# A four-layer graph transformer on one core: row sums taken from two key tiles added by an accumulating DMA, with one mask, one pool of large buffers and a new order table

## The chip, the core and the metric

The kernel runs on one core of one Trainium2 chip. A core has five engines with a queue each: TensorE (matmuls, PE in the profile), VectorE (DVE), ScalarE (ACT), GpSimd (POOL) and SyncE (SP, which here only issues transfers). Sixteen DMA engines move data between HBM and the on-chip memory SBUF, or within SBUF. Each queue runs in its own order; engines wait for one another through semaphores. The metric is the device time of one execution in microseconds (us).

## The reference, cut to what matters

Sixteen graphs of 1024 nodes with 256 features pass four attention layers that share one adjacency matrix. Layers 0, 1 and 3 are graph attention layers, layer 2 is a transformer layer. Only layer 2's attention is touched in its way of computing:

```python
# x: (16, 1024, 256), adj: (1024, 1024) int32, zeros and ones
h = jnp.maximum(_layernorm(x, axis=-1), 0.0)
x = x + _L0_gnn_ref(h, adj, W, a)            # masks with adj == 0
h = jnp.maximum(_layernorm(x, axis=-1), 0.0)
x = x + _L1_gnn_ref(h, adj, W, a)            # masks with adj > 0
h = jnp.maximum(_layernorm(x, axis=-1), 0.0)
x = x + _L2_gnn_ref(h, adj, ...)
...
def _L2_gnn_ref(x, adj, ...):                # 8 heads of 32 features
    scores = jnp.einsum('fnhd,fmhd->fhnm', q, k) / jnp.sqrt(D)
    scores = jnp.where(adj > 0, scores, -1e9)
    attn = jax.nn.softmax(scores, axis=-1)
    t = jnp.einsum('fhnm,fmhd->fnhd', attn, v).reshape(F, N, C)
    x = _layernorm(x + t, ln1_g, ln1_b)
    f_out = relu(x @ w1 + b1) @ w2 + b2
    return _layernorm(x + f_out, ln2_g, ln2_b)
```

The softmax is computed without subtracting a maximum: the exponentials are multiplied by a 0/1 mask, the weighted values and the sums of the weights are accumulated apart, and the values are multiplied by the inverse of the sums at the end.

## The kernel before

The kernel works in 64 stages, one for each layer and graph. `order` interleaves them so that the stages of different graphs fill one another's gaps: (2, b), (1, b+1), (3, b), (0, b+2) in the middle of the run. Everything that an engine does is laid down as an `op` with its engine, an assumed cost, what it comes after, and the buffers (`Hold`) that it takes and ends. `play` then plays all of them against those assumed costs and emits them in that order. Which op is preferred where several could go next comes from `RANKS`, a table of three characters for each op written out in the source. So the order of each queue is fixed when the kernel is built, by the table, the assumed costs and the number of buffers in each `Ring`.

A layer 2 stage has 32 items, one for each half of the queries `n` (512 of them), group of four heads `g` and key tile `j` (128 keys). `dot_item` lays one down:

- `scores` (L1522): four matmuls of 32 x 128 by 32 x 512 into two double banks of PSUM, one for each head (in the profile each f32 matmul appears as two instructions);
- two exponentials on ScalarE (L1536), two heads each, PSUM to the buffer `pe` in SBUF, 128 x 2048 f32, 1 MB;
- two multiplications by the mask on VectorE (L1544), in place;
- `values` (L1556): four matmuls, 32 columns each, that add v-transposed times `pe` into the bank `acc`, over the eight key tiles;
- in the same op the sums (L1561): four matmuls with `pick` as weights, 32 columns, column `g` ones and the others zeros, that add the column sums of `pe` into the bank `sums`, over the eight key tiles and both groups.

After the last key tile of a half, `dot_out` copies `acc` and `sums` to SBUF, transposes them (tps, tpo, L1587), inverts the sums, scales, adds into y (L1621, GpSimd), and `feed_forward` follows. Layer 3 (`pair_item`) has the same two kinds of matmul (L1402 values, L1426 sums), with its weights p2 from VectorE (L1368). Layers 0 and 1 use `gat_item` (av, L1312, weights L1295).

The large buffers of 1 MB lie in three rings: "p" with 4 (the weights), "big" with 4 (qT, kT of layer 2, r2 of layer 3), "y" with 2. Two masks of 128 x 8 x 1024 bytes, 1 MB each, are built at the start by `mask_of`: `mask_nz` (adj not zero, layer 0) and `mask_pos` (adj greater than zero, the others), each from 8 compares on VectorE (L1762, with a count of the neighbours, `degree`), 64 transposes on TensorE (L1768) and 8 copies on ScalarE (L1772). At the end some seen values are checked; if one is out of bounds a general path computes everything again, which these inputs do not need.

GpSimd's queue holds the inverse roots of the layer norms (L1010, L1011), adds into x and y, and before the change no transfer; nearly all transfers are issued on SP: x in (L623), out (L1501), the rows of source terms out to HBM (L1238, L1241) and back, spread over the partitions (L1252, L1257).

Of the kernel before, what the change touches and what calls it, by code (L numbers as in the profile page):

```python
# [28 lines left out]
U8 = mybir.dt.uint8  # L29
# [18 lines left out]
    "#&P#%+#&C#(I####%@#$p##d#$Y#%L#$g#%]#%q#&B#&3#&]#%M#'S#&`#'%#'Z#'q#&]#&T#%0#'[#'T#'>#(&#'j#(>#)W#)?#);#(X#)d#*$"  # L48
    "#(_#(##)6#);#'m#)=#)L#*x#)K#)W#)N#*0#*i#+@#)w#*m#,/#,h#,C#+[#+U#,p#,:#-P#,1#%8#&A#'b#$l#(N#%t#%>#&_#'N#%]#&Y#%Z"
    "#%{#'0#'q#%4#&6#'0#&[#&6#(j#&V#%F#'s#'T#'H#&F#(]#%x#'D#&(#%e#'Z#&{#&F#'i#&m#'9#'x#&W#'^#(6#'`#'>#'E#'g#'3#'@#(+"  # L50
    "#'8#(-#'D#*7#(V#(7#%/#?7#*X#'R#'>#'}#%V#)w#([#)<#+##<9#,@#Dm#B5#Db#EG#EA#,d#0v#)j#+s#&R#&i#(;#'W#(8#)3#(>#(R#'e"
    "#(q#):#(s#)6#+4#+7#+/#%z#)]#)u#).#(+#+'#*Y#*E#)?#+8#)@#(=#*1#,+#*M#+U#*0#+F#*|#+q#,$#+L#*8#+O#,;#+|#+9#-7#.|#,b"
    "#,O#.s#+W#.`#+-#.2#([#(b#(Y#)V#)_#*,#)z#(M#)Y#*A#*G#,-#.Y#,##/(#,f#+/#+r#+7#,f#.5#-)#)G#*A#,1#-:#-4#-?#-{#,[#.A"
    "#,|#+z#,R#-1#+G#-P#-|#.E#-w#05#)w#._#/W#/0#/7#.f#-}#-;#/u#-N#2`#Pu#41#0s#/]#0s#2k#1J#*D#*]#'-#'2##Z#)]#(@#*z#*M"
    "#(3#).#-)#(i#*E#(:#+r#*z#-o#2W#*B#,H#+T#&/#*:#);#+g#*J#,D#(t#)o#$+#){#+-#+1#)&#)U#*E#'w#*Q#)j#(N#'E#+@#,v#,^#*q"
    "#.T#';#)F#*j#+T#)c#-o#+I#,L#+P#GC#.h#).#*1#+t#,7#.8#,t#.M#,z#.e#//#11#/S#/]#-[#+w#+T#0J#/t#,;#.+#/%#-2#,f#,2#+E"
    "#3b#.o#.Q#/>#.)#0;#.`#.W#-d#36#.7#.+#02#0]#0t#0w#2T#1,#.>#1s#1_#4D#,X#04#16#0`#6S#2J#2r#1c#5|#0C#2O#2+#0K#-5#/{"
    "#.H#.w#-s#,Y#1S#3P#1G#1##1y#-O#0##2$#1C#1{#1=#1l#3n#2*#4P#3l#.=#2-#/a#27#2^#5+#25#0L#/c#2p#1r#0V#2d#5@#0T#4,#2N"
    "#42#4p#4p#4:#3_#33#5R#1J#3%#3+#e=#2(#5x#6$#5k#6M#8a#28#.:#0%#/n#-E#5e#4)#5%#/@#21#4l#2D#1<#4$#3d#2=#0r#2O#2*#2V"
    "#2p#/O#6/#-a#,(#3-#3N#4[#3^#49#8y#6%#41#4q#2*#12#0g#7]#18#5v#59#4}#6{#4]#3:#7d#4k#7r#2[#5C#2k#/t#2%#31#2&#3m#7e"  # L60
    "#3*#6Q#0P#3^#6-#4p#7f#27#4g#1,#5x#5*#6_#4N#5U#1k#7*#6z#52#8T#4]#7b#7`#3B#7k#7d#5E#6b#7Y#58#6##:,#5o#:j#:o#7Z#<:"
    "#83#:Q#;v#6|#6]#5{#4o#7##9i#7)#4S#9K#5o#7)#7.#88#=B#9k#1P#7V#4k#54#9e#7*#;W#9^#6Q#5f#7.#7)#:(#6C#6_#9T#6[#8h#9S"
    "#7&#<Q#6P#<F#:4#9b#8U#8i#8h#58#<F#=+#>7#5)#4L#7z#7-#:p#6m#9;#8Z#:u#;c#6W#<##:s#:T#<_#<{#<C#8t#:0#=>#<V#;*#;+#:6"
    "#9l#7M#<V#<k#=Z#:T#<Q#8J#7=#<:#88#Ac#;r#;j#=7#:A#;l#=g#=v#8t#;l#<t#>d#@?#='#:a#>X#<Y#=Q#=;#<e#A8#<&#9p#=R#=}#;Z"
    "#;F#9r#>L#@8#>B#=r#>1#90#=x#=z#?+#<j#?g#AL#@H#=f#?5#=t#<N#=u#;m#@%#@)#?+#?l#As#<p#?z#>V#?e#<_#BS#<W#@##Ar#?e#<]"
    "#;@#B{#?V#Bf#A(#?=#@W#At#?f#B8#B'#AF#EX#C0#A<#@f#Bg#A7#=*#@x#D7#BX#AY#Av#>o#DZ#C<#CI#C'#@V#@1#Ax#B_#AQ#CH#Ad#@i"
    "#BU#B$#DN#Cw#B)#@<#E0#BX#Ca#Eq#Dr#BU#EQ#C?#DO#EB#ED#Eb#F$#E>#F@#EL#Dw#Do#Ei#EF#Dq#Et#Ei#G$#Ei#Ff#FU#GK#I0#Fo#H+"
    "#FR#HB#H[#F0#HS#G^#JX#Ix#G)#Iy#J&#I0#J|#KV#JL#He#I`#Iy#KF#Ij#IY#M6#J0#Fm#G<#G[#KS#L7#O;#JJ#IJ#Mf#Km#MG#M4#LA#J{"
    "#KD#M9#K'#NN#Ln#Lz#M]#O+#OH#BO#BS#DY#AJ#C]#F)#Bq#B.#DY#D6#Dh#E[#B@#Ax#Dm#BX#CZ#EE#DG#E/#CO#CD#E0#BF#Db#G7#FK#C/"
    "#F(#EP#D|#D1#GB#FX#FP#F+#C%#>]#E9#CG#Fa#H2#Gn#GI#GX#FQ#FE#G4#H+#Eu#F/#Fi#EY#Gp#H;#Gk#E>#G&#I9#J+#H_#E:#Jw#Ht#Fy"  # L70
    "#H]#J>#EU#H9#H*#J,#H]#I(#J7#Ir#GQ#JL#I3#K,#G<#GF#J##I?#IR#K+#II#G}#IP#II#J?#IL#Ip#Mp#I9#Ho#E-#K.#JH#IM#KX#IY#K$"
    "#KN#K.#IU#Jf#KT#Lg#J^#KH#Jm#Kn#Jt#Jg#Ln#JN#K,#KM#Jd#I$#Ho#Nf#Mm#K1#N;#Me#LG#Mj#LU#M=#Oo#Pj#Jp#KE#O+#MD#N=#NC#Ld"
    "#LB#LY#NJ#NP#N.#OV#O}#N=#M%#OF#NO#N0#N;#O;#Om#OS#Pw#O_#O3#OR#M@#GZ#Mx#P.#JA#L3#PY#O7#Qf#OZ#NF#qD#Rw#Ot#QT#Yr#SN"
    "#|Q#>A#?E#99#;_#>G#:q#=]#?$#?,#6c#?B#<v#>W#<0#>9#Ax#=M#<z#<{#?f#=y#AF#AL#A/#@'#Cz#@p#@]#?5#@l#<l#AJ#BO#<i#@5#Cs"
    "#;?#?G#CN#=f#>'#=5#@j#A<#B+#@`#<w#E'#B[#Bk#DQ#BF#Af#Cd#D1#B>#lz#Ha#Bz#BA#HQ#JB#Mn#Fe#I]#J8#Ia#JV#IT#KW#Jg#L2#Im"
    "#Kt#M?#M7#Pn#P4#Q6#Ns#Is#N9#Qh#M]#OL#J/#N.#Io#PW#NR#MS#NQ#S=#JD#SW#Nq#Np#LG#Nt#N{#MN#LS#Q<#Qf#S_#Pp#P/#S_#N5#N'"
    "#Qw#TH#Nu#No#R8#MC#LI#MU#Q<#K|#Mb#LR#M9#L:#LK#OJ#O4#Q-#Pt#MM#Py#OW#S6#O%#NW#LM#O)#O(#QB#P_#P$#NY#St#Mr#L`#Or#Pa"
    "#Le#R5#O3#P>#O##R>#Q-#P5#OR#P)#Mr#Vx#Mh#RU#Q:#P|#RP#QN#P+#Sr$&C#_o#MW#Po#d:#_P#cS#P1#Qo#H]#Kc#O}#OP#Rx#NX#Qy#S,"
    "#R?#R,#QA#O&#Nq#Q4#X7#P`#S)#TD#SG#Tv#T[#Wm#T7#OP#Rh#Tq#Xv#UD#Q{#Te#Te#Ut#Ui#Wo#N_#TP#LF#RQ#Uq#RM#RX#Sf#VZ#Pd#Rc"
    "#TK#Q'#T*#R^#T9#U=#W3#R3#W?#U8#RR#UL#SU#]d#U}#VD#VW#VJ#Wb#Xv#eo#eE#p}#Wu#e|#ii#jv#ju#Y%#SG#W5#Ur#VY#T<#UF#W9#Sj"  # L80
    "#Ur#V-#[j#V+#U{#X5#Zq#Wh#Y-#TW#T0#WN#YD#Zi#Z-#WL#WX#X;#YO#Z9#XI#XG#Uo#[n#Y*#WC#ZV#Wc#Wi#_f#Xk#W<#Vp#W-#WY#T<#Yb"
    "#XD#[D#[X#Vc#X+#VR#YH#Qa#W_#Yu#V`#YZ#Vr#U`#[4#YN#Y$#^f#Zs#Y9#X$#Y>#Z8#Zm#W%#[J#Y'#V?#ZR#^X#ZV#Y|#ZJ#Ww#T/#^G#QI"
    "#^1#[;#Z0#[}#ZU#Z}#Z<#_h#WJ#Y$#[?#Z9#[r#^{#]]#Z+#]+#[|#ZD#^*#a5#Z^#Z5#^%#^M#]L#^a#]n#^g#]d#_r#^Y#]x#Yu#^p#]|#[W"
    "#^J#`1#aF#_n#ag#aE#bw#b.#b5#c<#c1#e/#a:#`+#^x#^^#`c#cZ#eB#`@#a^#c]#d@#f.#bC#eE#dv#_T#bV#`-#c@#cG#g(#bI#c'#d6#a<"
    "#g`#f_#f)#eE#f/#g?#gH#f`#gd#ge#gb#dD#hM#[l#]D#_@#Z}#^M#^f#Y_#_l#]h#Xg#X_#^B#[5#[L#^=#`O#]-#`%#[4#ZJ#[x#^%#]`#``"
    "#Z5#_'#^6#Z*#^b#``#^-#_T#^s#^C#^z#_h#^8#^.#a=#_L#`G#ag#]i#]5#`o#`m#_O#bT#`V#_6#_]#`o#a=#a8#^X#_Q#`X#`<#_O#_T#aB"
    "#_+#c%#`f#a2#`i#bd#_i#aQ#`,#_;#`9#a`#ap#`s#b,#^w#c7#d}#]}#b|#b@#`T#b?#c4#`v#`H#bI#bu#aw#aR#`u#b_#b/#ed#au#bE#ad"
    "#`t#c5#c<#dh#di#d@#dG#eE#cs#d-#fR#d/#e*#c{#ch#b%#dO#cx#ex#dO#e5#__#dK#fQ#e?#dC#e-#gB#hk#hR#eY#hw#i:#fO#g`#c,#ea"
    "#i%#f_#h7#jT#g1#ft#f8#ep#eA#hR#gB#hS#h{#fZ#hs#gx#j4#gC#dr#hR#ij#d|#bp#iI#k;#gu#i8#k##bE#h6#h<#gg#f+#iv#kK$1@#h|"
    "#ir#g-#lk#l$$<k#a>#bT#bM#bq#c&#bB#az#dG#b^#c.#cX#e##d3#f;#`g#fn#dU#e9#d[#bJ#fh#iY#cZ#dp#cv#e,#eg#e0#cS#dw#gl#e}"  # L90
    "#e*#e?#f.#fe#f%#e3#e:#be#fd#hA#fU#gg#d_#hF#kg#i<#f[#db#fD#bJ#b4#fU#i8#f^#h$#ei#fP#gt#h_#j/#gf#h;#d]#hQ#h0#j6#hE"
    "#l`#iF#lF#fC#h5#j<#kL#fd#gb#e|#b3#iC#hB#jH#j.#k_#hf#n_#h}#jw#hU#p*#kc#q4#uC#i'#pg#mV#ey#gu#iT#ht#kP#o^#k8#k8#gA"
    "#kl#nZ#lQ#kk#je#io#jd#h4#m9#k##iB#le#oP#jc#mq#p<#lT#m<#nA#n7#pc#s&#pS#m_#qx#pV#oD#l.#kl#l0#oZ#p_#qM#q<#oL#o7#qT"
    "#s+#md#pY#o6#n1#nP#s>#nE#nm#nd#rF#pZ#qk#p,#r##sj#p3#rB#rZ#uc$'C$(t$/$#ts$*R$'U$-S$/?#m3#nS#nK#k}#ni#n8#nR#q&#n="
    "#iK#iW#j}#l8#p1#on#q`#k-#oI#h6#rx#rJ#oS#rd#pa#q&#p1#nx#kd#n1#p^#mr#nb#oT#k?#lL#oD#mE#ot#m&#p3#nz#oR#o)#tw#ql#po"
    "#n,#mn#qQ#m,#lR#oQ#pZ#nm#n-#oB$7q#s3#oN#pv#oI#qY#pe#r##qK#n2#o(#r$#q}#m;#s*#td#od#t4#t(#t{#tV#s7#u@#oI#qz#tC#lV"
    "#vc#sG#v1#r[#t0#tb#uG#sJ#sM#wR#r;#s^#om#tP#tA#t[#qr#uN#n,#p-#tO#t9#ub#t/#v$#w4#ve#u9#uA#uN#r]#tF#ta#sE#v;#tX#oo"
    "#u5#qv#sO#ty#rJ#sR#t`#y0#vG#ra#s{#r(#s1#sh#w)#rb#w@#t*#rg#tu#tB#u*#t<#t(#sX#x%#tb#s>#u-#tN#u(#vo#v|#u*#wS#wQ#x&"
    "#vl#u'#xK#uS#xU#vd#v4#w3#xh#wx$Df$*w#wG#vC$'&$&6$'|#t0#t;#uB#rc#wB#vF#uX#s=#s9#uI#t`#xm#v@#v^#vI#v-#tm#uV#s}#t'"
    "#u{#u2#wZ#ws#t>#t?#xW#w4#y0#v_#vO#v<#x##t8#x8#wY#wg#vl#z1#ym#xh#y8#v2#u{#th#vo#yX#y5#yN#v@#zK#xi#xt#ub#yg#wr#wO"  # L100
    "#ze#wm#xl#y:#xZ#wm#yV#xr#xo#{v#yJ#yF#zH#y.#xq#yn#vZ#y`#zI#xV#x_#yy#wS#w)#{+#u_#}Q#{]#y`#za#xV#z.#{Y#zs#wH#xC#z%"
    "#zJ#{4#{1#{a#{4#zp#{X#{.#}Z$$q#{-#|$#|]#|f#|`#|X#z@#}'#{k#}%#}(#|[#xP#},#|:#|Q#|C$$D$%`$#f$#w$#O#}}$$%$#Z$$d$'y"
    "$&o$#z$$/$$,$$u$$f$%R$&=$$%$$9$$h$$]$$v$%|$'*$%[$$5$&e$%r$%Q$&A$*y$&Q$&I$'k$'b$)b$*0$([$(<$(y$)T$(^$(f$)m$*Z$*2"
    "$)5$*J#xz#}&#|L#zc#{?#|G#xZ#zX#zN#yp#z?#{d#y;#y}#|-#{[#|$#|o#z(#|;#{_#{6#|o#}J#{A#|m#{F#|K#|r#}I#|l#|f#}w#}9#}x"
# [488 lines left out]
def fast_path(tc, bad, x, adj, l0_w, l0_a, l1_w, l1_a, w_qkv, ln1_g, ln1_b, ln2_g, ln2_b, w1, b1, w2, b2, l3_w, l3_a, out):  # L593
# [13 lines left out]
    with ctx:  # L607
# [75 lines left out]


        flags = state.tile([P, NT * C], F32, tag="y0", bufs=1, name="flags").bitcast(BF16)
        rows_in = state.tile([P, 4, 2 * C], F32, tag="y1", bufs=1, name="rows_in")

        wx0, fill0 = gat_weights(None, [l0_w], flat(l0_a), ALPHA[0], "l0")

# [1213 lines left out]
```

## Time and profile before

| | us |
|---|---|
| time, median of 3 runs (4306.7 to 4307.0) | 4306.75 |
| span of the profiled execution | 4305.8 |
| TensorE idle in it | 59.5 |
| scores, L1522, 4096 instructions | 588.8 busy |
| values of layer 2, L1556, 4096 instructions | 552.6 busy |
| sums of layer 2, L1561, 4096 instructions | 540.9 busy |
| masks of layer 2, L1544, 1024 instructions of 1.24 | 1227.1 busy |
| exponentials of layer 2, L1536, 1024 of 1.022 | 994.8 busy |
| inverse roots on GpSimd, L1010 and L1011, 768 each | 292.2 and 549.4 busy |

The profile is one execution on the chip, so shares and single durations belong to its span, not to the median. Busy times of TensorE's groups overlap, since one matmul starts before the last has drained: the 4246.3 us that it is busy in all are less than its groups' sum. What a group costs is better read from the chain of waits, where the pieces stand end to end. A line such as "2068.00 0.86 PE sums L1561 x8" there says: from 2068.00 us of the span on, eight instructions of line 1561 held the chain for 0.86 us. In the groups, "out<-in", the shapes and the count are followed by the busy time and the mean duration in ns, then by the idle time of the engine before them and what ended it. In a table by stretches the columns are the stretch, its length, the busy time and count of TensorE, its weight loads, VectorE, ScalarE and GpSimd, the granted clock, the DMA share and GB/s. SPq stands for SyncE's queue, whose entries are issued transfers.

### The profile page before, as it was taken

How to read it: one execution, taken by the hardware profiler on the slowest of the kernel's cores; microseconds unless marked ns; L12 is line 12 of the kernel's file. 1: busy time of each engine (PE TensorE's matmuls, PEld its weight loads, DVE VectorE, ACT ScalarE, POOL GpSimd, SP SyncE). 2: the span in 40 equal slices, each digit the busy share in tenths (PEclk: the TensorE clock that was granted, in tenths of full speed). 3: DMA queues.
4: the chain of work that ended last, by engine and by line, in shares of the span. 5: the costliest groups of instructions: out<-in, count | busy, mean ns of one | idle time of the engine just before them, and what ended most of it. 6: DMA issues, size and time to landing. Idle time of an engine off the chain costs nothing.

```text
span 4305.8 us, 70159 instructions
## 1 busy us (share of the span) xinstructions
PE 4246.3 (99%) x28105; PEld 2207.6 (51%) x28105; DVE 3382.3 (79%) x5834; ACT 2006.0 (47%) x3091; POOL 1239.9 (29%) x2025
## 2 busy tenths in 40 slices
PE   8999999999999999999999999999999999999998
PEld 7735355553645536455354653545545455464433
DVE  7578877878778787787877878777787777858798
ACT  4462635536354363543535435354453634555351
POOL 3225131422314223142231422314232142333221
PEclk9999999999999999999999999999999999999999
DMA  3000000010000100000000000000000000000001
GB/s 112 6 6 25 21 21 30 1 45 6 21 30 1 45 6 20 30 13 33 6 26 26 21 25 6 25 26 21 26 6 26 25 21 30 1 30 1 21 10 41
DMA packets 59598, 96.05 MB, mean 22 GB/s; under 512 B 6281, under 2 KB 41473, under 8 KB 59265
## 3 DMA queue, kind: packets, MB, share of 16 engines
q1 hardware_dynamic: 58848, 90.98, 6.3%
q8 instruction: 222, 3.64, 0.4%
q14 instruction: 112, 0.91, 0.1%
q10 hardware_dynamic: 416, 0.52, 0.0%
HBM read 74.32 MB, written 17.17 MB: 21 GB/s over the span
## 4 chain that ended last, share of the span: by engine, by line
PE 92%; DVE 4%; ACT 1%; POOL 1%; issue 0%; DMA 0%; SPq 0%; DVEq 0%; ACTq 0%; POOLq 0%
PE pm L1037 21%; PE av L1312 21%; PE sc L1522 12%; PE acc L1556 10%; PE acc L1402 10%; PE sums L1561 9%; PE sums L1426 5%; PE tp L1030 3%; DVE pe L1544 2%; PE tpo L1587 1%; PE tpv L1465 1%; POOL v L1211 1%; DVE st L1006 0%; PE tps L1451 0%; PE tps L1587 0%
## 5 line engine op out<-in xcount | busy, mean ns | idle before, releaser
L1544 DVE TENSOR_TENSOR pe<-pe,mask_pos 128x1024 f32<-128x1024 f32 x1024 | 1227.1, 1240 | 240.2 <-ACT pe L1536 236.9
L1536 ACT ACTIVATE pe<-sc 128x1024 f32<-128x1024 f32 x1024 | 994.8, 1022 | 549.5 <-PE sc L1522 510.9
L1312 PE MATMUL av<-v,p 128*128 128x257 f32 x4096 | 939.9, 381 | 2.9 <-ACT o L1334 2.2
L1312 PEld LDWEIGHTS av<-v,p 128*128 128x128 f32 x4096 | 762.7, 190 | 150.5 <-issue 29.3
L1368 DVE SCALAR_TENSOR_TENSOR p<-r,e,mask_pos 128x1024 f32<-128x1024 f32 x512 | 623.0, 1275 | 134.1 <-DMA r<-kept 70.3
L1010 POOL TENSOR_SCALAR rstd<-stats 128x1 f32<-128x1 f32 x768 | 292.2, 381 | 1154.6 <-DVE stats L1007 1115.4
L1522 PE MATMUL sc<-qT,kT 32*128 32x512 f32 x4096 | 588.8, 639 | 1.1 <-ACT pe L1536 1.1
L1011 POOL TENSOR_TENSOR rstd<-rstd,minus_half 128x1 f32<-128x1 f32 x768 | 549.4, 715 | 63.9
L1556 PE MATMUL acc<-pe,v 128*32 128x512 f32 x4096 | 552.6, 603 | 0.2
L1561 PE MATMUL sums<-pe,pick 128*32 128x512 f32 x4096 | 540.9, 592 | 0.0
L1402 PE MATMUL acc<-p,v 128*32 128x512 f32 x4096 | 465.0, 594 | 0.0
L1037 PE MATMUL pm<-l_wx,hT 128*128 128x259 f32 (+1 forms) x1536 | 367.2, 387 | 2.8 <-ACT hT L1033 2.0
L1522 PEld LDWEIGHTS sc<-qT,kT 32*128 32x128 f32 x4096 | 162.7, 183 | 379.7 <-ACT pe L1536 239.2
L1621 POOL TENSOR_TENSOR y<-y,turned 128x512 f32<-128x512 f32 x64 | 90.1, 1428 | 820.4 <-DVE turned L1614 820.4
L1037 PEld LDWEIGHTS pm<-l_wx,hT 128*128 128x128 f32 x1536 | 286.9, 190 | 62.4 <-issue 14.3
L1561 PEld LDWEIGHTS sums<-pe,pick 128*32 128x32 f32 x4096 | 135.4, 110 | 304.6 <-issue 300.5
L1402 PEld LDWEIGHTS acc<-p,v 128*32 128x32 f32 x4096 | 133.2, 110 | 304.4 <-issue 279.4
L1006 DVE BATCH_NORM_STATS2 st<-x 128x6 f32<-128x256 f32 x512 | 213.4, 417 | 69.9 <-POOL x L1338 57.2
L1556 PEld LDWEIGHTS acc<-pe,v 128*32 128x32 f32 x4096 | 87.8, 108 | 350.4 <-issue 149.1
L1083 ACT ACTIVATE xn<-x,stats 128x256 f32<-128x256 f32 x256 | 121.5, 504 | 313.2 <-DVE stats L1007 267.5
L1426 PE MATMUL sums<-p,e 128*32 128x512 f32 x2048 | 245.0, 594 | 0.5 <-DVE rows_sb L1230 0.5
L1037 PE MATMUL pm<-hT,qkv_sb 128*128 128x512 f32 x512 | 229.8, 595 | 14.1 <-ACT hT L1033 14.1
(104 smaller groups left out, 4062.1 us busy)
## 6 DMA issues: line engine op xcount, KB each, us to landing
r<-kept SPq DMA_DIRECT2D x64, 512.0 KB
x<-in_x_dram SPq DMA_DIRECT2D x32, 512.0 KB
out_dram<-x SPq DMA_DIRECT2D x64, 256.0 KB
r<-kept SPq DMA_DIRECT2D x62, 256.0 KB
edges<-in_adj_dram SPq DMA_DIRECT2D x8, 512.0 KB
kept<-rows_sb SPq DMA_DIRECT2D x128, 2.0 KB
qkv_sb<-in_L_gnn_w_qkv_dram SPq DMA_DIRECT2D x1, 768.0 KB
rows_in<-in_L_gnn_a_dram SPq DMA_DIRECT2D x2, 256.0 KB
```

Source lines behind the costliest of these rows:

```text
L1010: nc.gpsimd.tensor_scalar(rh.t, mh.t[:, 1:2], EPS, None, ALU.add)
L1011: nc.gpsimd.tensor_tensor(rh.t, rh.t, minus_half, ALU.pow)
L1037: nc.tensor.matmul(dst, lhsT=lhsT[:, k, :], rhs=rhs[:, k, :], start=(k == 0), stop=(k == KC - 1))
L1312: nc.tensor.matmul(avh.t[:, : s.hs + 1], lhsT=phs[part].t[:, j % each, i * P : (i + 1) * P], rhs=s.v[:, j, h, :], start=(j == 0), stop=(j ...
L1368: nc.vector.scalar_tensor_tensor(ph.t[:, hh, :], s.rh[hp].t[:, hh, :], s.e[:, j, col : col + 1], mask_pos[:, j, :], ALU.max, ALU.mult)
L1402: nc.tensor.matmul(acc[n].t[(2 * hh + part) * W : (2 * hh + part + 1) * W, :], lhsT=s.v[:, jj, h, part * W : (part + 1) * W], rhs=p, start ...
L1426: both(lambda jj, n, hh, h, p: nc.tensor.matmul(sums.t[(2 * n + hh) * W : (2 * n + hh + 1) * W, 0, :], lhsT=s.e[:, jj, 2 * H + h : 2 * H + ...
L1522: nc.tensor.matmul(scs[pair].t[:, hh, :], lhsT=s.kh.t[r0 : r0 + D2, g, j * P : (j + 1) * P], rhs=s.qh.t[r0 : r0 + D2, g, cols], start=True ...
L1536: lambda pair=pair: nc.scalar.activation(part(pair), scs[pair].t, AF.Exp, scale=SCALE2),
L1544: lambda pair=pair: nc.vector.tensor_tensor(part(pair), part(pair), mask(), ALU.mult), [ex], tiles=True,
L1556: nc.tensor.matmul(head(acc, i), lhsT=s.v[:, j, g * QUAD + i, :D2], rhs=p(i), start=(j == 0), stop=(j == NT - 1))
L1561: nc.tensor.matmul(head(sums, i), lhsT=pick[:, g, :], rhs=p(i), start=(g == 0 and j == 0), stop=(g == KC - 1 and j == NT - 1),)
```

## The change

Four things change together.

The sums of a pair. `values` keeps its four matmuls for each key tile. The sums are no longer taken from each tile: after the odd tile of a pair, GpSimd issues a transfer that adds the odd tile's `pe` onto the even tile's, in SBUF, 128 x 2048 f32. It waits for the even tile's values matmuls and for the masks of both. `totals` then takes the sums from the even tile's buffer, four matmuls for two key tiles, as an op of its own, which waits for the transfer. The odd tile's buffer is released by its values and the transfer, the even tile's by the totals.

```diff
-                for i in range(QUAD):
-                    nc.tensor.matmul(
-                        head(sums, i), lhsT=pick[:, g, :], rhs=p(i),
-                        start=(g == 0 and j == 0), stop=(g == KC - 1 and j == NT - 1),
-                    )
...
             s.last_values = op(
-                PE, 1.715, at[0], values, masked + [s.vops[j]] + ([s.last_values] if j else []),
-                takes=takes, ends=[ph, s.vh], form=32,
+                PE, 0.8575, at[0], values, masked + [s.vops[j]] + ([s.last_values] if j else []),
+                takes=[] if j else [acc], ends=[ph, s.vh], form=32,
             )
...
+            if j % 2 == 0:
+                s.even = ph, s.last_values, masked
+                return
+            th, valued, ready = s.even
+
+            def gather():
+                nc.gpsimd.dma_start(
+                    out=th.t.rearrange("p i q -> p (i q)"), in_=ph.t.rearrange("p i q -> p (i q)"), accum_op=ALU.add
+                )
+
+            gathered = op(POOL, 1.0, at[0] - 4.0, gather, [valued] + ready + masked, ends=[ph], delay=8.0)
...
+            def totals():
+                for i in range(QUAD):
+                    nc.tensor.matmul(head(sums, i), lhsT=pick[:, g, :], rhs=th.t[:, i, :], start=first, stop=last)
+
+            s.last_sums = op(
+                PE, 0.8575, at[0] + 6.0, totals, [gathered] + ([] if first else [s.last_sums]),
+                takes=[sums] if first else [], ends=[th], form=32,
+            )
+            if last:
+                dot_out(s, n, sums, at[0] + 8.0)
```

One mask. `mask` (adj greater than zero) serves all layers. Where `mask_nz` was built, `negatives` counts on VectorE the entries below zero in each of the 8 tiles, with no transpose and no copy; the check at the end adds that there are none.

```diff
-        mask_nz = const.tile([P, NT, N], U8, name="mask_nz")
-        mask_pos = const.tile([P, NT, N], U8, name="mask_pos")
+        mask = const.tile([P, NT, N], U8, name="mask")
...
+            def count():
+                nc.vector.tensor_scalar(
+                    fh.t, edges[t // 2][:, t % 2, :], 0.0, 0.0, ALU.is_lt, ALU.add, accum_out=below[:, t : t + 1]
+                )
```

One pool. The rings "p", "big" and "y" become one set "m" of 11 buffers of 1 MB, any of which can hold any of the three kinds; weights and qT, kT, r2 are each still taken in the order in which they were laid down. The two banks of "acc" become a set of two as well.

```diff
-            "u": Ring(3, is_set=True), "acc": Ring(2, True), "p": Ring(4, True), "r": Ring(2, True), "y": Ring(2, is_set=True),
-            "big": Ring(4, True), "v0": Ring(1, True), "v1": Ring(1, True), "v2": Ring(1, True), "e": Ring(4),
+            "u": Ring(3, is_set=True), "acc": Ring(2, is_set=True), "m": Ring(11, is_set=True), "r": Ring(2, True),
+            "v0": Ring(1, True), "v1": Ring(1, True), "v2": Ring(1, True), "e": Ring(4),
```

A new table `RANKS`, longer by the new ops, and so a new order of every queue. In the changed kernel the masks of layer 2 are on line 1567, the values on 1576, the accumulating transfer on 1593, the sums on 1605, tps and tpo on 1624 and the inverse roots on 1034 and 1035.

## The prediction

> **What bounds the kernel now.** I read the busy times first, then the chain of waits in order of time, then the groups by line, then two short stretches for the price of a transfer.
>
> ```profile
> span 4305.8 us, 70159 instructions
> ...
> PE 4246.3 (99%) x28105; PEld 2207.6 (51%) x28105; DVE 3382.3 (79%) x5834; ACT 2006.0 (47%) x3091; POOL 1239.9 (29%) x2025
> ...
> DMA  3000000010000100000000000000000000000001
> ```
>
> TensorE is busy for all but 60 us of the span, at a granted clock of 0.998, and its queue is in order: what leaves it shortens the span, and what makes it wait lengthens the span, one for one. VectorE is second with 923 us idle. The DMA engines do next to nothing after the first slice. The chain of waits, in the attention stage (layer 2), shows what one item costs:
>
> ```profile
> 2067.00 1.00 PE acc L1556 x8
> 2068.00 0.86 PE sums L1561 x8
> 2068.86 1.07 PE sc L1522 x8
> 2069.93 0.99 PE acc L1556 x8
> ```
>
> Scores, values and row sums stand back to back: 1.07 + 1.00 + 0.86 = 2.93 us an item, 5.86 us for a pair of key tiles. The 0.14 us by which values cost more than sums is a change of tile form (32 rows to 32 columns); from columns back to full tiles costs about 0.19 us (16 av matmuls took 3.67 us right after such a change, 3.48 us without). The groups that matter beside these:
>
> ```profile
> L1544 DVE TENSOR_TENSOR pe<-pe,mask_pos 128x1024 f32<-128x1024 f32 x1024 | 1227.1, 1240 | 240.2 <-ACT pe L1536 236.9
> L1768 PE MATMUL tp_mask<-ident_b,flags 128*128 128x128 bf16 x128 | 10.0, 230 | 2.7 <-DVE flags L1762 2.2 <-ACT v L1172 0.5
> ```
>
> A pair of items needs four L1544 masks, 4 x 1.24 = 4.96 us of VectorE. The price of moving data, from the four 512 KB loads of r2 and from a small store whose successor waits for it:
>
> ```profile
> 384.50 2.64 SPq L1257 DMA_DIRECT2D r<-kept  x4
> ```
> ```profile
> 386.00:388.00 2.00, 2.00 (x11) 1.71 (x10) 0.61 (x2) 1.26 (x5) 1.00 (x3) 1.00 0.98 260
> 388.00:390.00 2.00, 1.46 (x10) 0.91 (x8) 1.45 (x2) 1.15 (x3) 0.52 (x1) 1.00 1.03 412
> 390.00:392.00 2.00, 1.43 (x7) 1.25 (x8) 2.00 (x3) 1.06 (x3) 0.00 (x0) 1.00 0.82 332
> 392.00:394.00 2.00, 2.00 (x11) 1.70 (x9) 1.75 (x2) 1.19 (x4) 0.00 (x0) 1.00 0.01 2
> ```
> ```profile
> 2058.76 0.63 SPq L1238 DMA_DIRECT2D kept<-rows_sb  x1
> ...
> 2060.52 0.82 SPq L1252 DMA_DIRECT2D r<-kept  x2
> ```
>
> The last two columns of the stretches are the DMA share and GB/s: with all 16 engines full a plain copy runs at 412 GB/s, 2.55 us for 1.05 MB. The 4 KB store was issued at 2058.76 and its reader at 2060.52: about 1.7 us is the fixed part of a transfer.
>
> **What leaves TensorE.** 512 items make 256 pairs, and each pair loses one group of sums: 256 x 0.86 = 220.2 us. In the new order the changes of tile form go from 525 to 550 into columns, 510 to 507 into rows, 232 to 263 into full tiles: 25 x 0.14 + 28 x 0.19 = 8.8 us back. Half of the mask transposes go: 10.0 / 2 = 5.0 us. Sum: 216.4 us less. Eight mask copies on ScalarE (1.015 us each) go off the path; VectorE's eight second compares become eight counts of the same 1.21 us.
>
> **What comes in: 256 accumulating transfers** of 128 x 2048 f32, 1.05 MB each, issued by GpSimd. The trace has none, so I bound one. Below: it costs the engines one pass, 2.55 us. Above: own data, other data and the result pass one after the other, 7.6 us. I take two passes, 5.1 us, as two operands must be read and the write can run beside them. GpSimd's own part is bounded by SP's issue (0.42 us for L1257, median) and GpSimd's costliest row (1.43 us, L1621); I take 1.0, nearer the latter, since even a copy of 128 x 8 elements takes GpSimd 1.24 us (L1211). From issue to data ready: 1.0 + 1.7 + 5.1 = 7.8 us.
>
> The Trainium skill states the same halving: in "Collectives: The Full Stack", section "The bandwidth ceiling: the fold count and why AG ≠ RS ≠ AR", a reduction is slower than a copy because both source reads go through one read ring, not because the addition costs anything. With the 435 GB/s fabric limit of "DMA: Bandwidth & Descriptors" ("Where 436 GB/s comes from"), two reads are an estimated 4.8 us and the final sum below would be 19 us lower. No run here shows an accumulating transfer.
>
> **Is it hidden?** The order of TensorE's queue, priced with the durations above, tells how much work stands between a pair's odd values and its sums: 7.5 us in the median, 5.0 at the 5th percentile. The masks run ahead too: those of the scores at 2051.10 ended at 2055.77, 5.3 us before their values began at 2061.08. So 7.8 us of latency alone is covered in most places. Two places are not covered, because one transfer fills all engines (share 0.98 to 1.03 above), so transfers queue.
>
> First, the dense run. Seven or so pairs of each stage follow each other every 2 x (1.07 + 1.00) + 0.86 = 5.0 us, and each wants 5.1 us of all 16 engines: even, with nothing to spare. The 0.1 us that adds up seven times is within the slack above; of a longer transfer the excess over 5.0 us counts seven times.
>
> Second, the end of each stage. In the usual stage, in us from its first scores, the even values of the last four pairs end at 102.1, 105.0, 108.8 and 110.5 (the gather waits for these), and the sums stand at 111.3, 112.1, 115.1 and 115.9. With O us per transfer the engines finish at 102.1 + O, + 2O, + 3O, + 4O, and the data is there 2.7 us (1.0 + 1.7) later. The last sums therefore wait, together with the waits before them, 102.1 + 4O + 2.7 - 115.9 = 4O - 11.1 us. O = 5.1: 9.3 us, 16 stages: 149 us. Until the last sums are in, dot_out cannot invert, so tps, tpo, the feed-forward and layer 3's inputs are late by the same time; this is TensorE's own delay, counted once.
>
> On GpSimd the waiting gather holds back what is queued behind it: in the dense run only the next gathers, at the stage's end the rstd pairs (L1010, L1011) and the adds into y and x. ScalarE's and VectorE's normalisations wait for those. GpSimd's L1010 idled 1115 us for VectorE before, so I charge nothing; without that cover it is 1.0 us of issue for each of the last four gathers, 64 us over 16 stages. A rule that speaks against the change: "SBUF — State Buffer", section "Who interferes with whom", has descriptor writing by GpSimd starved while VectorE is in a two-port mode; by the same section tensor_tensor takes only the read side, so by it L1544 delays nothing. Rows here show only that GpSimd's L1011 takes 0.715 us in the mean and 0.57 us beside VectorE's statistics.
>
> **VectorE.** 4.96 us a pair against TensorE's 5.0 in the dense run is a cover of 0.04 us; each 0.1 us more on L1544 would cost 0.36 us a pair, 40 us over 16 x 7 pairs. Just before the stage's end the values of four items pass in 6.7 us of TensorE work, while VectorE's queue has 8 masks at 1.24, two statistics at 0.60, two affine halves at 0.49 and two adds at 0.68: 13.5 us. The four items before leave it 1.4 us ahead, so up to 5.4 us a stage remain, 0 to 86 us; the scores stand up to four items ahead, from which the masks can start early, so I take a low value, 1 us a stage, 16 us.
>
> **The pool of 11 large buffers** (before 4 + 4 + 2; one mask less pays for the eleventh) costs nothing in itself: it is space, not work. The even tile is held until its sums, though: late transfers keep buffers from the next exponentials. That is the same backlog, not a second charge.
>
> **Sum.** 4305.8 - 216.4 + 149 + 16 = 4254.4 us of span; the median of the runs lies 1 us above the profiled span, so 4255 us, 1.2% below before.
>
> **Rivals.**
> 1. Transfers cheap (O = 2.55). For it: DMA is idle after the first slice, reads and writes may use separate paths. Against: two operands. Stall at the stage's end: the last pair is ready at 110.5 + 2.55 + 2.7 = 115.8, before 115.9, so none. 4305.8 - 216.4 + 16 + 1 = 4106 us.
> 2. The transfer rate takes TensorE's place (slower). Place: the sums at the end of each attention stage. Price: 4O - 11.1 plus 7 x (O - 5.0) a stage. At 7.6 us: 19.3 + 18.2 = 37.5 us, 600 us over 16 stages: 4707 us. It decides from 16 x (11O - 46.1) = 200, O = 5.3 us or 198 GB/s, only 4% above my value. For it: nothing in the trace shows that an addition runs at copy rate. Against: nothing either, except that the order leaves slack for latency.
> 3. VectorE becomes the bound. With L1544 0.1 us longer and the full 86 us, 4255 + 40 + 70 = 4365 us. For it: 0.04 us of cover. Against: it idles 923 us, and while TensorE waits for sums it catches up.
>
> **Chances.** Two reads, O between 4.6 and 5.6: 44%, giving 4305.8 - 216.4 + 16 + 1 + 117 = 4223 us up to, with 16 x 15.5 = 248, 4354 us (of this 28 faster, 5 the same, 11 slower). Cheap: 22%. Slower for good, by the rate (30%) or by VectorE (4%): 34%. Faster by over 0.2%: 50%; within 0.2%, which a measurement of this kernel can't tell from no change: 5%; slower: 45%. The likeliest case's own range is 4223 to 4354. For 8 in 10 I reach from the cheap case without VectorE's 16 us (4090) to the upper bound of the transfer (4710); half of the rate-bound case and a little of the cheap one lie outside.
>
> **What would show it.** L1605's sums at 2048 instructions instead of 4096, with TensorE's busy time near 4030. The accumulating queue's share: 256 x 5.1 us is 31% of the span at O = 5.1, 16% at 2.55, over 41% at 7.6. TensorE's waits for the transfer, none in the dense run, some 9 us at the end of each stage. VectorE's idle time before L1567 near zero in the dense run. I am wrong if an accumulating transfer is not about two copies long, or if waits stand in the dense run.

## The result, and the profile after

| | before | after |
|---|---|---|
| time, median, us | 4306.88 | 4342.49 |
| ratio after to before | | 1.0083, 95% interval 1.0069 to 1.0098 |
| span of the profiled execution, us | 4305.8 | 4344.9 |
| TensorE busy / idle, us | 4246.3 / 59.5 | 4143.8 / 201.1 |
| mean granted clock | 0.998 | 0.983 |

The change makes the kernel 0.8% slower. The time lies inside the range, 87 us above the forecast, and on the other side of the kernel before, whose median here is of four runs.

The page of the changed kernel, with the busy times, the DMA share over 40 slices and the queue of the accumulating transfers (packets, MB, share of 16 engines):

```profile
span 4344.9 us, 66664 instructions
...
PE 4143.8 (95%) x25993; PEld 2175.8 (50%) x25993; DVE 3368.5 (78%) x5836; ACT 2004.2 (46%) x3083; POOL 1408.4 (32%) x2281
...
DMA  3061805317053170531606235162350713435261
...
q0 software_dynamic: 36864, 268.45, 30.7%
```

TensorE is busy for 102 us less and idle for 142 us more. The transfers took 0.307 x 4344.9 / 256 = 5.21 us of all 16 engines each. The groups that answer to the sums, masks and values shown before:

```profile
L1567 DVE TENSOR_TENSOR pe<-pe,mask 128x1024 f32<-128x1024 f32 x1024 | 1206.9, 1233 | 190.5 <-ACT pe L1559 188.3
L1576 PE MATMUL acc<-pe,v 128*32 128x512 f32 x4096 | 543.0, 605 | 6.1 <-DVE pe L1567 4.7 <-ACT turned L1615 0.8
L1605 PE MATMUL sums<-pe,pick 128*32 128x512 f32 x2048 | 294.6, 637 | 127.2 <-DMA pe<-pe 126.4
L1593 POOL DMA_DIRECT2D pe<-pe x256 | 225.6, 888 | 976.8 <-PE acc L1576 669.5 <-DVE pe L1567 173.8 <-PE sc L1545 73.9
```

The new wait has a name: the sums sat 127.2 us, 126.4 of it for the transfer. The values hardly sat for the masks (4.7 us), which looks as if VectorE cost nothing; the experiments show otherwise. The end of one stage, first GpSimd's issues and then TensorE's queue on the timeline (start, us, engine, line, in brackets the idle time before and its releaser):

```profile
2931.86 0.92 POOL L1593 DMA_DIRECT2D pe<-pe  x1
2934.52 0.94 POOL L1593 DMA_DIRECT2D pe<-pe  x1
2936.49 0.85 POOL L1593 DMA_DIRECT2D pe<-pe  x1 [1.04 <-PE acc L1576]
2938.29 0.86 POOL L1593 DMA_DIRECT2D pe<-pe  x1 [0.94 <-PE acc L1576]
```
```profile
2944.15 1.93 PE L1605 MATMUL sums<-pe,pick 128*32 128x512 f32 x8 [4.13 <-DMA pe<-pe]
2949.27 1.93 PE L1605 MATMUL sums<-pe,pick 128*32 128x512 f32 x8 [3.18 <-DMA pe<-pe]
2951.13 1.97 PE L1054 MATMUL tp<-ident,xn 128*128 128x128 f32 x8
2956.15 1.34 PE L1605 MATMUL sums<-pe,pick 128*32 128x512 f32 x8 [3.05 <-DMA pe<-pe]
```

Four transfers are issued within 6.4 us, and the first two sums shown start 5.1 us apart: the data comes at the engines' pace, not GpSimd's. The three waits make 10.4 us in this stage, the most of all sixteen: the 64 waits of the span come to 126.4 us, 7.9 us a stage, with those at the end of first halves counted in. The sums at 2944.15 take 1.93 us where 1.06 is usual: the clock, to which the last section returns.

### The profile page after: what moved, and what is told of

It is laid out like the page before. It is cut to its first block, busy times and chain, and to the rows that moved or that the text cites. A ratio compares the mean times of both kernels' runs of the same rounds, so it can differ in the third digit from the quotient of the medians.

```text
span 4344.9 us, 66664 instructions
## 1 busy us (share of the span) xinstructions
PE 4143.8 (95%) x25993; PEld 2175.8 (50%) x25993; DVE 3368.5 (78%) x5836; ACT 2004.2 (46%) x3083; POOL 1408.4 (32%) x2281
## 3 DMA queue, kind: packets, MB, share of 16 engines
q0 software_dynamic: 36864, 268.45, 30.7%
## 5 line engine op out<-in xcount | busy, mean ns | idle before, releaser
L1567 DVE TENSOR_TENSOR pe<-pe,mask 128x1024 f32<-128x1024 f32 x1024 | 1206.9, 1233 | 190.5 <-ACT pe L1559 188.3
L1335 PE MATMUL av<-v,p 128*128 128x257 f32 x4096 | 966.8, 387 | 8.5 <-DVE p L1318 6.1
L1391 DVE SCALAR_TENSOR_TENSOR p<-r,e,mask 128x1024 f32<-128x1024 f32 x512 | 621.9, 1274 | 95.7 <-DMA r<-kept 85.8
L1545 PE MATMUL sc<-qT,kT 32*128 32x512 f32 x4096 | 626.3, 645 | 2.5 <-ACT pe L1559 2.5
L1035 POOL TENSOR_TENSOR rstd<-rstd,minus_half 128x1 f32<-128x1 f32 x768 | 565.5, 736 | 64.0
L1593 POOL DMA_DIRECT2D pe<-pe x256 | 225.6, 888 | 976.8 <-PE acc L1576 669.5
L1425 PE MATMUL acc<-p,v 128*32 128x512 f32 x4096 | 465.9, 593 | 0.0
L1605 PE MATMUL sums<-pe,pick 128*32 128x512 f32 x2048 | 294.6, 637 | 127.2 <-DMA pe<-pe 126.4
L1545 PEld LDWEIGHTS sc<-qT,kT 32*128 32x128 f32 x4096 | 192.6, 184 | 388.8 <-issue 184.4
L1318 DVE SCALAR_TENSOR_TENSOR p<-r,e,mask 128x512 f32<-128x512 f32 x512 | 359.2, 755 | 6.8 <-DMA r<-kept 6.4
L1361 POOL TENSOR_TENSOR x<-x,o 128x256 f32<-128x256 f32 x128 | 100.6, 787 | 570.4 <-ACT o L1357 570.1
L1425 PEld LDWEIGHTS acc<-p,v 128*32 128x32 f32 x4096 | 132.1, 110 | 293.1 <-issue 277.4
L1449 PE MATMUL sums<-p,e 128*32 128x512 f32 x2048 | 247.5, 593 | 0.3 <-DVE p L1391 0.3
```

Of the source, the lines that this page charges most:

```text
L1035: nc.gpsimd.tensor_tensor(rh.t, rh.t, minus_half, ALU.pow)
L1318: nc.vector.scalar_tensor_tensor(ph.t[:, j % each, :], rh.t, s.e[:, j, H + h : H + h + 1], mask[:, j, cols], ALU.max, ALU.mult)
L1335: nc.tensor.matmul(avh.t[:, : s.hs + 1], lhsT=phs[part].t[:, j % each, i * P : (i + 1) * P], rhs=s.v[:, j, h, :], start=(j == 0), stop=(j ...
L1391: nc.vector.scalar_tensor_tensor(ph.t[:, hh, :], s.rh[hp].t[:, hh, :], s.e[:, j, col : col + 1], mask[:, j, :], ALU.max, ALU.mult)
L1425: nc.tensor.matmul(acc[n].t[(2 * hh + part) * W : (2 * hh + part + 1) * W, :], lhsT=s.v[:, jj, h, part * W : (part + 1) * W], rhs=p, start ...
L1545: nc.tensor.matmul(scs[pair].t[:, hh, :], lhsT=s.kh.t[r0 : r0 + D2, g, j * P : (j + 1) * P], rhs=s.qh.t[r0 : r0 + D2, g, cols], start=True ...
```

## The experiments

Each median stands against the kernel before on the same chip (4306.6 to 4307.6 us). First theory: the transfers' rate costs all that was lost against the 4106 us of cheap transfers.

**1 to 3: the size and the kind of the transfer.**

```diff
-    out=th.t.rearrange("p i q -> p (i q)"), in_=ph.t.rearrange("p i q -> p (i q)"), accum_op=ALU.add
+    out=th.t.rearrange("p i q -> p (i q)")[:, :256], in_=ph.t.rearrange("p i q -> p (i q)")[:, :256], accum_op=ALU.add
```

The second run has 1024 in place of 256; the third leaves `accum_op` away and copies all 2048 columns.

> The transfer adds only the first 256 of 2048 columns (the row sums are then incomplete); every instruction, its place and its wait are as in the changed kernel. Theory (the rate of the accumulating transfer, 5.1 us of all engines each, makes TensorE wait, and the waits drop its clock): about 0.6 us per transfer, no wait for it at TensorE, granted clock back at 0.998, 4090 to 4120 us. Rival A (the new order, one mask and VectorE cost it): no gain, 4300 to 4345 us. Rival B (the fixed part, GpSimd's issue and the landing, costs it): waits for the transfer stay, 4200 to 4340 us.

> The transfer adds the first 1024 of 2048 columns (row sums incomplete). Theory: 2.55 us per transfer, half the share of the queue (15 to 16%), 4100 to 4135 us, at most 20 us above the 256-column run. Rival A and B: within 20 us of the changed kernel or of the 256-column run's own high value.

> The transfer copies the odd tile over the even one, 2048 columns, without adding (the row sums then count the odd tile alone). Theory (two reads set the rate): 2.55 us per transfer, 15 to 16% of the engines, landing in 5 to 6 us, time within 15 us of the 1024-column run. Rival (bytes written or the number of packets set it, or GpSimd's own descriptor work): landing 8 us and 4320 to 4345 us as with the addition.

| | us | ratio, interval | share of the engines | us each | landing, us |
|---|---|---|---|---|---|
| add 256 columns | 4204.7 | 0.9761, 0.9744 to 0.9777 | 5.4% | 0.89 | 2.7 |
| add 1024 columns | 4204.6 | 0.9759, 0.9743 to 0.9776 | 16.8% | 2.76 | 4.6 |
| copy 2048 columns | 4198.4 | 0.9749, 0.9733 to 0.9766 | 16.3% | 2.67 | 4.6 |
| add 2048 columns (the change) | 4342.5 | 1.0083, 1.0069 to 1.0098 | 30.7% | 5.21 | 8.1 |

"Us each" is the share times the span over 256. The line of each queue in the page, for the copy and for the addition of 1024 columns:

```profile
q0 software_dynamic: 36864, 268.45, 16.3%
```
```profile
q0 software_dynamic: 36864, 134.23, 16.8%
```

The addition takes as long as a copy of twice the bytes, as taken in the prediction; that the second half of its time is a second read is not shown by these runs. Up to 2.8 us a transfer costs hardly anything (the copy took 4198.4 us, and run 5, without any transfer, 4198.3), and from there to 5.2 us comes 138 us. The copy landed in 4.6 us, a little earlier than the 5 to 6 expected. But the first two times lie above what their theory gave (4090 to 4135 us), and all lie far above the 4106 us of cheap transfers. The 4204.7 us of the first fall into the range of rival B, yet the sums waited only 2.1 us for transfers in that run, so the fixed part of a transfer is not the reason. About 100 us are lost elsewhere.

**4: fewer transfers at the stage's end.** The last three pairs of each stage sum both tiles directly, 48 transfers fewer, 41 us more of TensorE.

```diff
+        DIRECT = lambda n, g, j: n == NH - 1 and g == KC - 1 and j > 1
...
+                held = [th, ph] if direct else [th]
+                for u, h in enumerate(held):
+                    for i in range(QUAD):
+                        nc.tensor.matmul(
+                            head(sums, i), lhsT=pick[:, g, :], rhs=h.t[:, i, :],
+                            start=first and u == 0, stop=last and u == len(held) - 1,
+                        )
```

> The last three pairs of each attention stage take their sums from both tiles directly, as before the change, without a transfer (13 transfers a stage instead of 16); the output is complete. TensorE's work grows by 48 x 0.86 = 41 us less a few form changes. Theory (transfers queue at the stage's end): about two thirds of the waits and of the lost clock go, 4190 to 4260 us. Rival A (order and VectorE): 4342 + 38 = about 4380 us.

4297.3 us, ratio 0.9974 (0.9963 to 0.9986): 45 us under the change, less than the theory wanted and more than rival A did. TensorE's sums sat 38.5 us for transfers instead of 126.4. 4297.3 - 41 is 4256, still 52 above the runs with small transfers.

**5 to 7: no transfer, and a lighter VectorE.** The transfer is left out in the first two; in the last two each mask multiplication covers half the queries.

```diff
-    nc.gpsimd.dma_start(out=..., in_=..., accum_op=ALU.add)
+    pass
```
```diff
-    masks = lambda: mask[:, j, n * HALF : (n + 1) * HALF].unsqueeze(1).to_broadcast([P, 2, HALF])
+    masks = lambda: mask[:, j, n * HALF : n * HALF + 256].unsqueeze(1).to_broadcast([P, 2, 256])
...
-    nc.vector.tensor_tensor(part(pair), part(pair), masks(), ALU.mult), [ex]
+    nc.vector.tensor_tensor(part(pair)[:, :, :256], part(pair)[:, :, :256], masks(), ALU.mult), [ex]
```

> Leaves out all 256 accumulating transfers; the row sums are then taken from the even key tiles alone. Order of every queue as in the changed kernel. Theory (what is left of the loss when transfers are small, about 100 us over the predicted 4106, sits in the new order and in VectorE's masks): 4185 to 4205 us, as with a transfer of 256 columns (4204.7). Rival (the latency of a transfer, issue to landing, costs those 100 us however small it is): 4100 to 4130 us.

> As the kernel without transfers, and each mask multiplication of layer 2 covers 256 of its 512 queries, so that VectorE spends about 0.6 us less on each of 1024 (some 620 us in all). Leaves out half of the masking too. Theory (VectorE's masks are late and hold the values): 4090 to 4130 us. Rival (the order itself costs it: groups that stand alone and wait for a semaphore or a change of form): no more than 20 us under the kernel without transfers, 4170 to 4205 us.

> The changed kernel with all its transfers, but each mask multiplication of layer 2 covers 256 of its 512 queries. Leaves out half of the masking. Theory (two separate losses: the transfer rate 138 us, which stays, and VectorE's lateness up to 100 us, which goes): 4245 to 4290 us. Rival (late masks are hidden behind the queue of transfers, so the rate decides alone): 4320 to 4345 us.

Without transfers 4198.3 us (0.9745, 0.9729 to 0.9762): the theory's range; latency has no part in the 100 us. With half the masks besides, 4162.8 (0.9665, 0.9648 to 0.9681): 35 us less, between theory and rival. With all transfers and half the masks it takes 4317.8 (1.0026, 1.0017 to 1.0036): 25 us under the change, again between the two. So the masks take a part, some 57 us over the 4106 remain with half of them, and the transfers cost 144 us (4342.5 - 4198.3) with full masks and 155 with half.

**8: the last pair of each half directly.**

```diff
-        DIRECT = lambda n, g, j: n == NH - 1 and g == KC - 1 and j > 1
+        DIRECT = lambda n, g, j: g == KC - 1 and j == NT - 1
```

> The last pair of each half (both halves of the queries) takes its sums directly from both tiles: 32 transfers fewer, 32 groups of sums more (27.5 us of TensorE). Output complete. Theory (the queue of transfers at the end of each half is one transfer too long): one transfer of 5.2 us less at each end, 16 to 32 ends, 4342 + 28 - 83 to 4342 + 28 - 130, so 4240 to 4290 us. Rival (the wait only moves to the pair before): 4320 to 4370 us.

4456.6 us (1.0347, 1.0330 to 1.0364), slower than anything expected. The wait for transfers did fall, to 75.8 us. But layer 3's values (L1425) and sums (L1449), which sat 0.0 and 0.3 us in the changed kernel, now sit 23.9 and 23.3, mostly for VectorE's weights. The table of ranks was made for one set of operations and costs: a small edit of these gives another order in every queue. So this run does not test the rate, and run 4, whose order moved too, is only a bound.

**9 and 11: the old order with the same work removed.** This undoes everything but the missing sums: the kernel before, its order, its rings, both masks, and the sums taken from the odd tiles alone.

```diff
-    for i in range(QUAD):
+    for i in range(QUAD if j % 2 else 0):
         nc.tensor.matmul(
             head(sums, i), lhsT=pick[:, g, :], rhs=p(i),
-            start=(g == 0 and j == 0), stop=(g == KC - 1 and j == NT - 1),
+            start=(g == 0 and j == 1), stop=(g == KC - 1 and j == NT - 1),
         )
```

> The kernel before, with its own order, pools and two masks, but the row sums taken from the odd key tiles alone: 256 groups of sums fewer and no transfers. Leaves out the even tiles' part of the row sums. Theory (the new order is what keeps the kernel with hardly any transfer at 4198 instead of 4106): 4307 - 220 plus up to 20, so 4085 to 4110 us. Rival (with 220 us less on TensorE its waits for masks and exponentials show up in any order): 4160 to 4200 us.

4206.0 us (0.9766, 0.9750 to 0.9783): the rival, 6 us above its range. The same 220 us of sums leave TensorE, in the old order and without a transfer, and the time falls by 101 us only. The next run adds the half masks of above to it.

> The kernel before in its own order, row sums from the odd key tiles alone (as in the run that took 4206.0) and each mask multiplication of layer 2 over 256 of its 512 queries. Leaves out the even tiles' part of the row sums and half of the masking. Theory (of the 220 us that leave TensorE about 117 come back as waits, because VectorE's masks are then the next limit, also in the old order): 4110 to 4160 us. Rival (other waits, of transposes and of ScalarE, take it back): 4185 to 4206 us.

4115.9 us (0.9554, 0.9538 to 0.9570): the theory. Halving VectorE's masks gives back 90 of the 119 us that had not come out. The waits of TensorE agree. These are the rows of the values before, in the old order with half the sums (with a transpose that also waits for VectorE), and with half the masks too:

```profile
L1556 PE MATMUL acc<-pe,v 128*32 128x512 f32 x4096 | 552.6, 603 | 0.2
```
```profile
L1556 PE MATMUL acc<-pe,v 128*32 128x512 f32 x4096 | 576.6, 604 | 23.5 <-DVE pe L1544 22.0
...
L1030 PE MATMUL tp<-ident,y 128*128 128x128 f32 x512 | 71.3, 276 | 22.2 <-DVE y L1021 21.8 <-ACT y L1063 0.2
```
```profile
L1556 PE MATMUL acc<-pe,v 128*32 128x512 f32 x4096 | 538.2, 603 | 0.0
```

The transpose's wait falls from 21.8 to 1.4 us in the last run. The half masks were not tried with all sums in place; there the values sat 0.2 us in all, so hardly any wait for a mask shows.

For the 29 us that are left the traces show another place. A pair of items in the dense run, with half the masks, in the chain of waits:

```profile
1978.20 1.24 PE sc L1522 x8
1979.44 1.00 PE acc L1556 x8
1980.44 0.86 PE sums L1561 x8
1981.30 1.07 PE sc L1522 x8
1982.37 1.00 PE acc L1556 x8
```

That is 5.17 us where the prediction has 2 x (1.07 + 1.00) + 0.86 = 5.0: one of the two groups of scores takes 1.24 us in place of 1.07. No wait shows here: TensorE is busy all the time, VectorE 11.09 of 20 us. Over the span the scores are busy 621.8 us, 588.8 before, with the same 4096 instructions:

```profile
L1522 PE MATMUL sc<-qT,kT 32*128 32x512 f32 x4096 | 621.8, 639 | 0.9 <-ACT pe L1536 0.8
```

These 33 us are about the size of the 29; what makes the scores longer is not shown. In the new order the scores show the same (618.6 us without transfers).

Where VectorE holds TensorE is seen in one stretch of a stage, 82 to 102 us after its first values, around its last ones, in the table by stretches (stretch, length, busy time and count of TensorE, weight loads, VectorE, ScalarE and GpSimd, clock, DMA share, GB/s). Before, with the 20 us ahead of it:

```profile
2100.00:2120.00 20.00, 19.96 (x132) 8.09 (x128) 18.41 (x27) 10.05 (x11) 3.57 (x8) 1.00 0.00 1
2120.00:2140.00 20.00, 20.00 (x172) 5.18 (x172) 19.44 (x28) 12.91 (x15) 13.50 (x14) 1.00 0.01 2
```

The old order with half the sums, then with half the masks too:

```profile
2077.00:2097.00 20.00, 18.36 (x128) 6.06 (x121) 19.69 (x30) 11.10 (x15) 12.18 (x12) 1.00 0.00 1
```
```profile
2033.00:2053.00 20.00, 19.26 (x140) 10.19 (x137) 17.23 (x35) 9.96 (x14) 9.21 (x11) 1.00 0.00 1
```

The changed kernel without transfers, then the changed kernel, here with its dense run and the end of the first half too:

```profile
2063.00:2083.00 20.00, 18.11 (x119) 6.35 (x112) 19.55 (x35) 6.78 (x12) 12.67 (x16) 1.00 0.00 0
```
```profile
2069.00:2089.00 20.00, 20.00 (x160) 5.45 (x160) 17.97 (x16) 15.90 (x17) 3.43 (x4) 1.00 1.01 217
2089.00:2109.00 20.00, 18.89 (x148) 5.55 (x140) 15.65 (x25) 13.20 (x15) 6.87 (x10) 1.00 0.86 174
...
2129.00:2149.00 20.00, 16.21 (x108) 5.10 (x104) 19.48 (x34) 6.39 (x9) 14.10 (x19) 1.00 1.02 205
```

The third busy time is VectorE's. Before the change it already worked 19.44 of these 20 us. What TensorE no longer has to do there becomes a wait (20.00 to 18.36). With the masks halved VectorE has room and TensorE is nearly full again. In the changed kernel a full DMA queue (1.02) comes on top. Much of the loss does not even show as idle time: from before to the run with half the sums TensorE's busy time falls by 151 us, not 220, and its idle time grows by 50. Part of the waits counts as busy, since the ends of matmuls are modelled: with half the masks TensorE runs the same 26057 instructions, and its busy time falls by another 41 us (4095.5 to 4054.1), its idle time by 49.

**10: the halved clock.** Twelve matmuls with zero weights, which wait for no transfer, ahead of each of the last two sums of a stage.

```diff
+    if n == NH - 1 and g == KC - 1 and j > NT - 4:
+        for i in range(3 * QUAD):
+            nc.tensor.matmul(head(sums, i % QUAD), lhsT=none, rhs=qkv_sb[:, 0, :HALF], start=False, stop=False)
```

> The changed kernel, complete, with 12 more matmuls of 128 x 32 by 128 x 512 with zero weights (2.6 us at the full clock) ahead of each of the last two groups of sums of a stage, which do not wait for the transfer: 32 times, 82 us of TensorE if nothing hid them. Theory (the waits there are 3 us and more and the halved clock after them costs part of the 44 us): the time at half clock falls from 151 us to under 100 us and the kernel takes 4315 to 4345 us. Rival (the halved clock costs nothing, as the work at half speed only fills waits that come anyway): 4342 to 4380 us.

4359.4 us (1.0120, 1.0103 to 1.0136): the rival's range. The time at half clock fell from 151 to 96 us, as the theory had it, yet the kernel is 17 us slower. 65 of the 82 us of added work do not show in the time: they stood in waits, or the shorter time at half clock paid for them. What the halved clock costs by itself is not settled by this; keeping TensorE warm does not pay here.

**12 and 13: another order.** Every queue's order written out as a plain list, made with the planner's costs and with the transfers counted as one queue of 5.3 us each.

```diff
+            o = min((o for some in open_ops for o in some), key=lambda o: key[o.number])
...
+                if o.eng == POOL and o.delay == 8.0:
+                    moved = max(moved, at + 1.8) + 5.3
+                    end = moved + 0.2
```

The last one also takes 57 of the 256 pairs directly, from a set of op numbers `DIRECT`, and has its own list.

> The changed kernel, complete, all 256 transfers, the same operations; only the order of every queue is another: written out as a plain list, made with the transfers counted as a queue of 5.3 us each. Theory (the 138 us of the transfer queue are a matter of where the sums stand; other stages' work can stand before them): 4215 to 4265 us. Rival (the transfers' rate decides, whatever the order): 4320 to 4345 us.

> As the reordered kernel, with an order of its own, and 57 of the 256 pairs sum both tiles directly, without a transfer (57 x 0.86 = 49 us more of TensorE). Output complete. Theory (the engines of the transfers are relieved where pairs stand dense, which frees more than the 49 us): 4180 to 4235 us, below the reordered kernel with all transfers. Rival (with a better order nothing is left to free): 4255 to 4300 us, above it.

Reordered, all transfers: 4325.7 us (1.0045, 1.0028 to 1.0061), in the rival's range. The sums' wait for transfers falls from 126.4 to 83.9 us, but that of the values for the masks grows from 4.7 to 22.7:

```profile
L1566 PE MATMUL acc<-pe,v 128*32 128x512 f32 x4096 | 556.7, 613 | 24.3 <-DVE pe L1557 22.7
...
L1595 PE MATMUL sums<-pe,pick 128*32 128x512 f32 x2048 | 290.7, 626 | 84.0 <-DMA pe<-pe 83.9
```

Another order gave 17 us back of 144; whether a better one exists stays open. With 57 pairs taken directly: 4275.8 us (0.9929, 0.9913 to 0.9946), above the theory's range but below the reordered kernel, which the rival did not expect, and faster than the kernels before and after the change:

```profile
L1607 PE MATMUL sums<-pe,pick 128*32 128x512 f32 x2504 | 326.2, 606 | 61.4 <-DMA pe<-pe 60.8
```

Its list was made anew, and that of the kernel before was not, so what part of its 0.7% comes from the transfers is not shown.

## Why the prediction was wrong, step by step

**The step that failed** is the opening one, that what leaves TensorE's queue shortens the span one for one, and in the sum the term "VectorE: +16 us", with its bounds of 0 to 86. The forecast without the transfers' 149 us is 4106 us; without transfers the changed kernel takes 4198.3, 92 us more. In the old order the same work removed gives 101 of 220 us. Halving the masks gives back 90 of the other 119, which is 5.6 us a stage: the upper bound of 5.4 us was the better value than the 1 us taken. The reason given for the low value, that the masks can start early since scores stand up to four items ahead, fails in the stretch above, at the stage's end: VectorE was busy 19.44 of 20 us there before the change, so it has no time in which to start early. "It idles 923 us" was true of the span and not of that stretch.

In the new order the account is less complete. Of the 92 us, halved masks give back 35, not 90, and the scores, busy 618.6 us and not 588.8, would account for some 30; the other 27 or so are open. With masks halved in both, the new order without transfers takes 47 us more than the old one (4162.8 to 4115.9); with full masks the two are about even (4198.3 to 4206.0). Of the 47 us, 20 are idle time of TensorE (80.1 to 60.6), and transposes that wait for ScalarE's xn have 21.1 us of it against 9.9. The rest was not taken apart; the pool of 11 buffers and the single mask, which belong to these kernels, were not tried alone.

**Work leaving TensorE**, 216 us, was too large by about 30. L1605 has 2048 instructions as expected, but with the masks halved the old order gave 192 of its 220 us: a group of sums was priced at its 0.86 us, and the scores beside it were taken to stay at 1.07.

**The transfer**: 5.1 us expected, 5.21 measured; landing 7.8 and 8.1; GpSimd's issue 1.0 and 0.89. The rule that a reduction is halved by its two reads (the Trainium skill, "Collectives: The Full Stack", section "The bandwidth ceiling: the fold count and why AG ≠ RS ≠ AR") agrees with the addition's 5.21 us against the copy's 2.67. GpSimd's issue is hardly shorter with half the masks (881 ns against 888), so VectorE's masks do not delay it to speak of, as assumed.

**The stage's end**: 149 us expected, 144 measured by leaving the transfers out. The mechanism was right, the closeness is in part luck: the sums' waits make 126.4 us, 7.9 a stage where 9.3 were worked out (the stage shown has 10.4), some of them stand at the end of the first half, and the halved clock, which the prediction did not have, is in the 144.

**The dense run** was even, as said: TensorE busy 20.00 of 20 us under a DMA share of 1.01. But the transfers take 5.21 us and not 5.1, and a pair takes TensorE 5.16 us (from the scores at 2069.97 to those at 2075.13) and not 5.0: two misses that cancel. Not foreseen was the end of the first half, where TensorE loses 1.1 of 20 us (18.89) and the kernel without transfers none:

```profile
2023.00:2043.00 20.00, 20.00 (x156) 6.29 (x156) 16.45 (x27) 13.98 (x17) 5.69 (x10) 1.00 0.01 2
```

**TensorE's busy time** was to be near 4030 and is 4143.8; without transfers it is 4103.2. Waits that count as busy, the longer scores and the time at half clock all add to it; how much each was not measured.

**The signs** named in the prediction did not help: the sums' count and the queue's share came as said, VectorE's idle time in the dense run was 2.0 of 20 us and not near zero, and neither sign of being wrong appeared. None of them looked at the term that failed.

**The rivals**: cheap transfers are refuted by the 5.21 us, the 7.6 us of the longer transfer too. The third, VectorE, came nearest with 4365 us, at a chance of 4%. It had the right engine and, in its 86 us at the stage's end, the right place; its other 40 us, from longer masks, did not come (L1567 takes 1.233 us, L1544 took 1.240), so the nearness is in part luck.

## What to carry to other kernels

Work taken from the bounding engine is worth no more than what the second engine leaves free in the same stretch. So price a removal from the table by stretches: an engine at 97% there, as VectorE was here, is the bound as soon as the first gets lighter, whatever its share of the span says. And look at the neighbours of what is removed: the scores beside the missing sums took 1.24 us in place of 1.07. An addition by transfer cost twice a copy; where such transfers come closer together than their length, the last of them arrives late by the sum of what is missing, and neither lighter masks (155 us in place of 144) nor another order (17 us back) took much of that away here.

## What was not expected of the hardware

The granted clock fell to 0.5 in pieces of 3.41 us or multiples of it (but for the last piece of each span), mostly after waits of a few us: 151 us in 28 pieces in the changed kernel, 16 us in 2 before. The same stage end as above, by stretches (the clock is third from the end):

```profile
2945.00:2950.00 5.00, 1.82 (x12) 0.20 (x8) 4.97 (x9) 0.92 (x2) 4.44 (x8) 0.50 1.03 211
...
2964.60:2968.00 3.40, 3.40 (x17) 2.92 (x16) 3.25 (x6) 0.43 (x2) 2.68 (x2) 1.00 0.00 0
```

TensorE was busy 1.82 of 5 us there, and the sums in it took 1.93 us instead of 1.06. The prediction left this out, though the Trainium skill, "TensorE: Matmul & The Clock Gate", section "What's actually happening", states a fall to half speed after one idle window of about 3.4 us; the pieces of 3.41 us agree with that length. The time ahead of a piece need not be idle all through, though: in the 3.41 us before the 28 pieces TensorE was busy for 0.94 us in the mean, and only before four of them not at all.
